# Attention outputs of two batches together, and the output products as seven products added in place

## The chip, the cores and the metric

The kernel runs on one core of one Trainium2 chip. The metric is device microseconds of one execution, from three runs before the change: a median of 2983.91 us, from 2983.39 to 2986.14.

A core has five engines that run side by side, each with its own queue, worked off in order: TensorE (PE in the profile; its weight loads are PEld), VectorE (DVE), ScalarE (ACT), GpSimd (POOL) and SyncE (SP), from which this kernel issues all its transfers. An instruction that needs another engine's result waits for a semaphore, and everything behind it in its own queue waits too. In this kernel TensorE's products go to tiles in PSUM, from where VectorE and ScalarE read them; everything else lies in SBUF.

## The reference

Two layers of masked attention with a residual and a normalisation each, over 128 batches of 128 rows and 512 columns in float32. Layer 0 has 4 heads and layer 1 has 8, each of 64 columns:

```python
q = split_heads(x @ Wq); k = split_heads(x @ Wk); v = split_heads(x @ Wv)
sim = jnp.einsum('bhid,bhjd->bhij', q, k) * scale
sim = jnp.where(adjacency_mask[:, None, :, :], sim, neg)
attn = jax.nn.softmax(sim, axis=-1)
out = jnp.einsum('bhij,bhjd->bhid', attn, v)          # heads joined: 256 columns
x = _layernorm(x + (out @ Wo + bo))                   # layer 0
# layer 1: h = layernorm(x) * gamma + beta, qkv = h @ w_qkv.T, 8 heads (512 columns),
# the mask also admits the diagonal
x = _layernorm(x + (out1 @ w_out.T + b_out))
```

The products that matter here are the last of each layer: `out @ Wo`, for each batch a 128x256 by 256x512 product in layer 0 and a 128x512 by 512x512 product in layer 1.

## The kernel before

Two batches make a group g (G = 2), so there are NG = 64 groups. The function `step(s)` works at several groups at once, as a pipeline: the projections of layer 0 for group s, attention of layer 0 for group s-1, the qk projection of layer 1 for group s-2, and attention of layer 1 for group s-3. A step has two halves, k = 2s and 2s+1, one for each batch of the groups. The order of instructions on every engine is the order in which the Python code issues them (a manual schedule): what stands earlier in `step` stands earlier in each engine's queue.

The projections are already formed by a scheme that multiplies two 2x2 block matrices with seven block products instead of eight. The left matrix's blocks are the two batches (rows) and the two halves of the inner dimension (columns); the right one's blocks are the halves of the weight. `sums` (L257) makes four sums of the left blocks on GpSimd (L266), the weights' sums are made once at the start (`weight_sums`, L160). `product` (L275) issues the products of layer 1 (kinds "qk" and "v", matmuls at L304) and `product_0` (L337) those of layer 0 (L361). The products are numbered 1 to 7, and the table `INTO` says to which accumulator each goes: 1, 6, 7 and 4 all run on in accumulator "a", 5 and 3 in "f", 2 in "c". The accumulator is read between them: after products 1, 5 and 6 ScalarE copies the partial sum out (`e`, `eqk`, `ev`; L330, L371), after 4 it copies the result (L332, L373), and after 2, 3 and 7 VectorE adds a copied partial sum and writes the result (L335, L376). A product that goes on in an accumulator has to wait until the copy of the one before it has been made.

In each half, for both layers: `scores(k)` makes the score products (L400) into four PSUM tiles, GpSimd fills the score tile with the masked value (L410), VectorE selects scores by the mask (L412), takes the row maxima (L415), and ScalarE makes the exponentials and their sums (L424). At its end `scores` calls `exponentials(1)`, which issues the exponentials of layer 0 at once; those of layer 1 wait for the next `exponentials()`. `normalised` has VectorE's reciprocal (L432) and GpSimd's multiplication (L433). `blocks` transposes the probabilities in 32x32 blocks (L448) and puts them out to memory (L198), `probs_arrive` fetches them back with the blocks in order (L204). `attend(k-1)` multiplies them with v (L471), half a step later, and copies the result (L474).

`residual` (L487) is the output product: for each batch and layer, two or four 128x512 matmuls into one PSUM tile (L493), then VectorE adds the residual (L499) and takes mean and variance (L501, L503), GpSimd makes the roots (L506 to L517), and `norms` (L522), issued by the next `flush()`, normalises on VectorE (L524). `addend` has prepared the residual with the bias (L483, L484). Layer 0's result is transposed (`turn`, L214), put out and fetched back (`arrive`), and `finish` (L245) scales it into layer 1's input; `in_order` does the same for x. Layer 1's result goes out (L528).

PSUM: a rotating pool of five tiles (`mm_tile`) serves scores, attention, the "c" accumulators and the output products; three single tiles serve the other accumulators ("a", "a0" and "f").

Of the kernel before, what the change touches and what calls it, by code (L numbers as in the profile page):

```python
# [17 lines left out]
P = 128  # L18
# [9 lines left out]
def kernel(ctx: ExitStack, tc: tile.TileContext, x, adj, wq, wk, wv, wo, bo,  # L28
# [13 lines left out]
    four = ctx.enter_context(tc.tile_pool(name="four", bufs=4))  # L42
    dram = ctx.enter_context(tc.tile_pool(name="dram", bufs=2, space=bass.MemoryType.DRAM))
    ps_mm = ctx.enter_context(tc.tile_pool(name="ps_mm", bufs=5, space=PSUM))
# [20 lines left out]
    X, M = {}, {}  # L65

    def load(g):
        if g >= NG:
            return
        X[g] = four.tile([P, G, E], F32, tag="x", name=f"x_{g}")  # L70
        M[g] = four.tile([P, G, N], U8, tag="m", bufs=6, name=f"m_{g}")
        nc.sync.dma_start(X[g], x[g * G:(g + 1) * G].rearrange("b n e -> n b e"))
        nc.sync.dma_start(M[g], adj[g * G:(g + 1) * G].rearrange("b i j -> i b j"))
# [8 lines left out]
    mhalf = const.tile([P, 2], F32, name="mhalf")  # L82
# [25 lines left out]

    spare = []
    for tag, n in (("qk1", 4), ("v1", 2), ("xT1", 2), ("xs1", 2)):  # L110
        rows_n = one.tile([P, n, E], F32, tag=tag, name=f"raw_{tag}")
        spare.extend(rows_n[:, i] for i in range(n))

    def load_transposed(dst, src, name, scaled=0):
        rows, cols = src.shape
        raws = []
        for r in range(rows // P):
            if not spare:
                raw = three.tile([P, cols], F32, tag="h", bufs=7, name=f"{name}_{r}")
            else:  # L120
                raw = spare.pop(0)
            nc.sync.dma_start(raw, src[r * P:(r + 1) * P, :])
            raws.append(raw)
# [36 lines left out]
    def weight_sums():  # L160
        for w, ws in ((w1qk, wsqk), (w1v, wsv)):
            for c in range(KH):
# [6 lines left out]
                t2, t3, t4 = ws[:, 0, c], ws[:, 1, c], ws[:, 2, c]  # L169
                nc.vector.tensor_sub(t3, b22, b12)  # L170
                nc.vector.tensor_sub(b12, b12, b11)
                nc.vector.tensor_sub(t2, b22, b12)
                nc.vector.tensor_sub(t4, b21, t2)

    def weight_sums_0():
        b11, b12, b21, b22 = (w0[:, c:c + KH, h].rearrange("p c t f -> p c (t f)")
                              for c in (0, KH) for h in range(2))
        t2, t3, t4 = (ws0[:, i].rearrange("p c t f -> p c (t f)") for i in range(3))
# [4 lines left out]

    weight_sums_0()
    load_transposed(w1, w_qkv, "w_qkv", scaled=INNER[1])
    setup.append(turn_gamma_beta)
    load_transposed(wo1, w_out, "w_out")
    setup.append(weight_sums)

    WO = (wo0, wo1)  # L190
    RATIO, H, XT, QK, V, QKV = {}, {}, {}, {}, {}, {}
# [14 lines left out]
    TURNED, SCR, RAW = {}, {}, {}  # L206

    def turn(l, g, b):
        if not 0 <= g < NG:
            return  # L210
        if b == 0:
            TURNED[l] = one.tile([P, 4, G * KC * 32], F32, tag=f"turned{l}", name=f"turned{l}_{g}")
        src = X[g][:, b] if l == 0 else H[g, b]
        nc.vector.transpose(TURNED[l].rearrange("p a (b c i) -> p a b c i", b=G, c=KC)[:, :, b],  # L214
                            src.rearrange("p (c a i) -> p a c i", a=4, i=32))
        if b == G - 1:
            SCR[l] = put(TURNED[l], f"scr{l}_{g}")

    def arrive(l, g):
        if not 0 <= g < NG:  # L220
            return
        RAW[l] = one.tile([P, 4, G, KC, 32], F32, tag=f"raw{l}", name=f"raw{l}_{g}")
        fetch(RAW[l].rearrange("p a b c i -> p a (b c i)"), SCR[l])

    def first_transposed():
        xT = XT[0, 0] = one.tile([P, KC, T], F32, tag="xT0", name="xT0_0")
        for b in range(G):
            pt = mm_tile(f"xt_{b}")
            for c in range(KC):
                nc.tensor.transpose(pt[:, c * N:(c + 1) * N], X[0][:, b, c * P:(c + 1) * P], ident)  # L230
# [26 lines left out]
    def sums(l, g):  # L257
        xT = XT[l, g]
        xs = one.tile([P, 4, KH, N], F32, tag=f"xs{l}", name=f"xs{l}_{g}")
        a = xT.rearrange("p (h c) (b n) -> p b h c n", h=2, b=2)  # L260
# [6 lines left out]
        XS[l, g] = xs  # L267
# [69 lines left out]
    def product_0(g, *which):  # L337
# [5 lines left out]
        for i in which:  # L343
# [10 lines left out]
            elif first:  # L354
                tag = {"a": "a0", "f": "f"}[bank]
                ACC[0, bank] = ps_st.tile([P, 512], F32, tag=tag, name=f"{bank}0_{g}")
# [273 lines left out]
```

## Time and profile before

| what | value |
|---|---|
| profiled execution, device time | 2984.46 us |
| its span, first to last instruction | 2982.7 us |
| time around the span | 1.8 us |
| mean granted TensorE clock | 0.994 of full speed |
| busy: PE / PEld | 2920.0 / 2402.9 us |
| busy: DVE / ACT / POOL | 1854.0 / 1334.2 / 1567.4 us |
| output matmuls (L493) | 1536 records, 713.2 us busy, mean 600 ns |
| period of a step in the steady part | 45.14 us |

A row of a timeline gives start and length in us, the engine, the line of kernel.py, the operation, what it writes and reads with partitions x elements, the number of instructions merged in the row, and in brackets for how long the engine sat idle ahead of it and who ended that wait. TensorE's records come in pairs: an fp32 matmul of the program leaves two, so "x4" on an output row of 128x512 is two matmuls of the program. Matmuls overlap and their ends are modelled, so the distance between two starts says what one costs.

### The profile page before, as it was taken

To read this page: it belongs to the slowest core of one execution; us is meant where nothing else is said; L and a number is where in the kernel's file an instruction comes from. 1 tells how busy PE (TensorE), PEld (TensorE's weight loads), DVE (VectorE), ACT (ScalarE), POOL (GpSimd) and SP (SyncE) were. 2 spreads that over 40 slices of the span, in tenths; PEclk is the share of its full clock that TensorE was granted. 3 is DMA by queue.
4 is the path that set the end of the run, shared out by engine and by line. 5 is a ranking of instruction groups with operands and counts; after the bars stand their busy time and mean duration, and the time that the engine had idled before them with its cause. 6 is when DMAs were issued, how large, how long until landed. Compare 5 with 4: busy or idle time off the path is not lost.

```text
span 2982.7 us, 59421 instructions
## 1 busy us (share of the span) xinstructions
PE 2920.0 (98%) x22089; PEld 2402.9 (81%) x22089; DVE 1854.0 (62%) x3291; ACT 1334.2 (45%) x4619; POOL 1567.4 (53%) x2055
## 2 busy tenths in 40 slices
PE   6899999999999999999999999999999999999997
PEld 5788888888888888888888888888888888888865
DVE  4466666666666666666656666666666666666654
ACT  2344444444444444444544444444444444444442
POOL 2455545545545555555555555455455455455543
PEclk8999999999999999999999999999999999999999
DMA  5454544544544544544544545545445445445332
GB/s 170 123 149 129 150 141 127 161 136 124 165 135 125 165 136 127 160 134 134 156 132 140 150 131 147 146 129 153 141 126 161 137 122 168 133 125 163 118 100 89
DMA packets 249136, 414.42 MB, mean 139 GB/s; under 512 B 41608, under 2 KB 181392, under 8 KB 248848
## 3 DMA queue, kind: packets, MB, share of 16 engines
q1 hardware_dynamic: 248848, 410.62, 46.3%
q8 instruction: 175, 2.87, 0.4%
q14 instruction: 113, 0.93, 0.1%
HBM read 209.72 MB, written 200.80 MB: 138 GB/s over the span
## 4 chain that ended last, share of the span: by engine, by line
PE 96%; DVE 1%; DMA 1%; ACT 1%; issue 0%; POOL 0%; SPq 0%; POOLq 0%; DVEq 0%; ACTq 0%
PE o L493 22%; PE qka L304 15%; PE a L361 12%; PE qkf L304 8%; PE va L304 8%; PE sc L400 6%; PE av L471 6%; PE f L361 6%; PE qkc L304 4%; PE vf L304 4%; PE c L361 3%; PE vc L304 2%; ACT sm L424 1%; DMA scrp<-turned 0%; DMA pT<-scrp 0%
## 5 line engine op out<-in xcount | busy, mean ns | idle before, releaser
L424 ACT ACTIVATE sm<-sm,nmax 128x128 f32<-128x128 f32 x1536 | 595.2, 389 | 618.6 <-DVE nmax L415 604.9
L493 PE MATMUL o<-wo,aT 128*128 128x512 f32 x1536 | 713.2, 600 | 10.0 <-ACT aT L474 10.0
L506 POOL TENSOR_SCALAR ve<-mv 128x1 f32<-128x1 f32 x256 | 57.0, 223 | 1133.0 <-DVE rec L432 798.8
L493 PEld LDWEIGHTS o<-wo,aT 128*128 128x128 f32 x1536 | 278.3, 191 | 269.3 <-issue 246.8
L433 POOL TENSOR_TENSOR sm<-sm,rec 128x512 f32<-128x512 f32 (+1 forms) x256 | 397.0, 1561 | 171.9 <-DVE rec L432 171.9
L412 DVE COPY_PREDICATED sm<-m,sc 128x512 f32<-128x512 uint8 (+1 forms) x512 | 271.0, 581 | 29.1 <-POOL sm L410 7.0
L424 ACT ACTIVATION_READ_ACCUMULATOR sm<-sm,nmax 128x1 f32 x1536 | 288.0, 187 | 0.0
L448 DVE STREAM_TRANSPOSE turned<-sm 128x512 f32<-128x512 f32 (+1 forms) x256 | 246.0, 965 | 45.0 <-POOL sm L433 45.0
L304 PE MATMUL qkf<-xs,w 128*128 128x128 f32 x2048 | 249.9, 275 | 0.1
L304 PE MATMUL qka<-xs,wsqk 128*128 128x128 f32 x2048 | 249.6, 275 | 0.0
L415 DVE TENSOR_REDUCE nmax<-sm 128x4 f32<-128x512 f32 (+1 forms) x256 | 244.0, 953 | 8.8
L304 PEld LDWEIGHTS qkf<-xs,w 128*128 128x128 f32 x2048 | 239.0, 192 | 0.6 <-POOL xs L266 0.4
L304 PEld LDWEIGHTS qka<-xs,wsqk 128*128 128x128 f32 x2048 | 239.0, 192 | 0.0
L524 DVE TENSOR_SCALAR h<-h,mv,rstd 128x512 f32<-128x512 f32 x128 | 70.0, 547 | 265.0 <-POOL rstd L513 265.0
L432 DVE RECIPROCAL rec<-total 128x4 f32<-128x4 f32 (+1 forms) x256 | 44.7, 175 | 296.6 <-ACT sm L424 296.6
L266 POOL TENSOR_TENSOR xs<-xT 128x256 f32<-128x256 f32 x256 | 186.0, 727 | 34.4 <-PE w_qkvt L129 14.5
L410 POOL MEMSET sm<- 128x512 f32 (+1 forms) x256 | 181.1, 735 | 1.4 <-DVE turned L448 1.3
L330 ACT COPY ev<-va 128x256 f32<-128x256 f32 x128 | 47.6, 372 | 298.7 <-PE va L304 298.7
L513 POOL TENSOR_TENSOR rstd<-ve,mhalf 128x2 f32<-128x2 f32 (+1 forms) x256 | 165.9, 648 | 21.3
L330 ACT COPY eqk<-qka 128x512 f32<-128x512 f32 x128 | 75.1, 587 | 214.4 <-PE qka L304 214.4
L484 POOL TENSOR_TENSOR h<-h,bias 128x512 f32<-128x512 f32 x128 | 162.7, 1271 | 7.0 <-ACT h L483 6.9
L484 POOL TENSOR_TENSOR x<-x,bias 128x512 f32<-128x512 f32 x128 | 162.2, 1267 | 0.0
(122 smaller groups left out, 5825.5 us busy)
## 6 DMA issues: line engine op xcount, KB each, us to landing
scrp<-turned SPq DMA_DIRECT2D x124, 768.0 KB, 3.3
pT<-scrp SPq DMA_DIRECT2D x496, 192.0 KB, 4.0
scr<-turned SPq DMA_DIRECT2D x127, 512.0 KB, 2.7
raw<-scr SPq DMA_DIRECT2D x508, 128.0 KB, 3.0
x<-in_x_dram SPq DMA_DIRECT2D x64, 512.0 KB, 4.2
out_dram<-y SPq DMA_DIRECT2D x128, 256.0 KB, 2.0
m<-in_adj_dram SPq DMA_DIRECT2D x64, 32.0 KB, 4.0
scrp<-turned SPq DMA_DIRECT2D x4, 512.0 KB, 3.2
```

The lines of the kernel that those rows point to most:

```text
L266: nc.gpsimd.tensor_tensor(o, a0, a1, op=op)
L304: nc.tensor.matmul(o, lhsT, rhs, start=first and n == 0, stop=n == len(todo) - 1, skip_group_check=True)
L361: nc.tensor.matmul(acc[:, t * P:(t + 1) * P], lhsT, rhs, start=first and n == 0, stop=n == len(todo) - 1, skip_group_check=True)
L400: nc.tensor.matmul(ps[h % 2][:, h // 2, :], q_, k_, start=True, stop=True)
L410: nc.gpsimd.memset(sm, (NEG0, NEG1)[l])
L412: nc.vector.copy_predicated(sm[:, s], mask[:, None, :].to_broadcast([P, K, N]), ps[s][:, :K, :])
L415: nc.vector.tensor_reduce(nmax, sm, AX.X, ALU.max, negate=True)
L424: nc.scalar.activation(sm[:, s, k, :], sm[:, s, k, :], AF.Exp, bias=nmax[:, s, k:k + 1], accum_out=total[:, s, k:k + 1])
L433: nc.gpsimd.tensor_tensor(sm, sm, rec[:, :, :, None].to_broadcast([P, 2, K, N]), op=ALU.mult)
L448: nc.vector.transpose(t[:, :, lo:hi, :], sm)
L484: nc.gpsimd.tensor_tensor(xin, xin, (bias0, bias1)[l], op=ALU.add)
L493: nc.tensor.matmul(pm, aT[:, c * P:(c + 1) * P], WO[l][:, c, :], start=(c == 0), stop=(c == nk - 1))
```

## The change

Attention of a group is now made for both batches at one place, `attend(s)`, for layer 0 of group s-2 and layer 1 of group s-4, so each layer's outputs come later by up to a step, and there is one more step. The output products take the same seven-product form as the projections (`out_product`): GpSimd makes the four sums of the attention outputs (`out_sums`), each product has one (layer 0) or two (layer 1) 128x256 matmuls, and after each product VectorE adds the accumulator, as it stands, into one quarter of the residual tile R, in place. The residual tile is the one in which x was loaded, and it stays one tile through both layers (six buffers of two batches). Mean and variance are taken per batch (`stats`), the roots for both batches together (`roots`); layer 1 is normalised on ScalarE (`norms_1`), layer 0 on VectorE (`norms_0`). The pool of rotating PSUM tiles has four tiles instead of five, and there is a fourth accumulator tile ("f0").

In `step` the order is new: product_0's parts stand between the output products of layer 0, both row transposes of a group are made together, product_0's number 7 and the statistics, `blocks`, normalisation and `turn` stand ahead of the second half's scores, and v's first four products stand behind these scores; the copies of their partial sums stand ahead of the exponentials of layer 1, and behind those of layer 0.

```diff
-    four = ctx.enter_context(tc.tile_pool(name="four", bufs=4))
+    six = ctx.enter_context(tc.tile_pool(name="six", bufs=6))
-    ps_mm = ctx.enter_context(tc.tile_pool(name="ps_mm", bufs=5, space=PSUM))
+    ps_mm = ctx.enter_context(tc.tile_pool(name="ps_mm", bufs=4, space=PSUM))
...
+    spare = []
+    def spare_rows(pool, tag, n):
+        rows_n = pool.tile([P, n, E], F32, tag=tag, name=f"raw_{tag}_{len(spare)}")
+        spare.extend(rows_n[:, i] for i in range(n))
+    for i in range(4):
+        spare_rows(six, "r", 2)
+    for tag, n in (("qk1", 4), ("v1", 2), ("xT1", 2)):
+        spare_rows(one, tag, n)
-        X[g] = four.tile([P, G, E], F32, tag="x", name=f"x_{g}")
-        M[g] = four.tile([P, G, N], U8, tag="m", bufs=6, name=f"m_{g}")
-        nc.sync.dma_start(X[g], x[g * G:(g + 1) * G].rearrange("b n e -> n b e"))
+        R[g] = six.tile([P, G, E], F32, tag="r", name=f"r_{g}")
+        M[g] = six.tile([P, G, N], U8, tag="m", name=f"m_{g}")
+        nc.sync.dma_start(R[g], x[g * G:(g + 1) * G].rearrange("b n e -> n b e"))
...
+    WSO = tuple(const.tile([P, 3, i // P // 2, E // 2], F32, name=f"wso{l}") for l, i in enumerate(INNER))
+    def weight_sums_out(l):
+        hk = INNER[l] // P // 2
+        w = (wo0, wo1)[l]
+        combine(*(w[:, c:c + hk, h * E // 2:(h + 1) * E // 2] for c in (0, hk) for h in range(2)),
+                *(WSO[l][:, i] for i in range(3)))
...
+    setup.append(weight_sums)
+    setup.append(lambda: weight_sums_out(0))
-    setup.append(weight_sums)
+    setup.append(lambda: weight_sums_out(1))
...
+    def turn(l, g):
+        if not 0 <= g < NG:
+            return
+        t = one.tile([P, 4, G * KC * 32], F32, tag="turned_in", name=f"turned{l}_{g}")
+        for b in range(G):
+            nc.vector.transpose(t.rearrange("p a (b c i) -> p a b c i", b=G, c=KC)[:, :, b],
+                                R[g][:, b].rearrange("p (c a i) -> p a c i", a=4, i=32))
+        SCR[l] = put(t, f"scr{l}_{g}")
+        RAW[l] = one.tile([P, 4, G, KC, 32], F32, tag="raw", name=f"raw{l}_{g}")
...
+        xs = XS[l, g] = one.tile([P, 4, KH, N], F32, tag=f"xs{l}", name=f"xs{l}_{g}")
+        halves_sums(xs, XT[l, g].rearrange("p (h c) (b n) -> p b h c n", h=2, b=2))
+    def halves_sums(xs, a):
         s1, s2, s3, s4 = (xs[:, i] for i in range(4))
         for o, a0, a1, op in ((s1, a[:, 1, 0], a[:, 1, 1], ALU.add),
                               (s2, s1, a[:, 0, 0], ALU.subtract),
                               (s4, a[:, 0, 1], s2, ALU.subtract),
                               (s3, a[:, 0, 0], a[:, 1, 0], ALU.subtract)):
             nc.gpsimd.tensor_tensor(o, a0, a1, op=op)
-        XS[l, g] = xs
...
-                tag = {"a": "a0", "f": "f"}[bank]
-                ACC[0, bank] = ps_st.tile([P, 512], F32, tag=tag, name=f"{bank}0_{g}")
+                ACC[0, bank] = ps_st.tile([P, 512], F32, tag=f"{bank}0", name=f"{bank}0_{g}")
-                e = one.tile([P, 512], F32, tag=("e5_0" if i == 5 else f"e{i}"), name=f"e0_{i}_{g}")
-                EV[0, i] = e[:, :3 * P]
+                EV[0, i] = one.tile([P, 3 * P], F32, tag=f"e0_{i}", name=f"e0_{i}_{g}")
...
+    def out_product(l, g, *which):
+        if not 0 <= g < NG:
+            return
+        aT, so = AT[l, g], SO[l, g]
+        hk = INNER[l] // P // 2
+        w, ws = WO[l], WSO[l]
+        EH = E // 2
+        for i in which:
+            left = {1: aT[:, 0, :hk], 2: aT[:, 0, hk:], 3: so[:, 3], 4: aT[:, 1, hk:], 5: so[:, 0],
+                    6: so[:, 1], 7: so[:, 2]}[i]
+            right = {1: w[:, :hk, :EH], 2: w[:, hk:, :EH], 3: w[:, hk:, EH:], 4: ws[:, 2],
+                     5: w[:, :hk, EH:], 6: ws[:, 0], 7: ws[:, 1]}[i]
+            bank, first = INTO[i]
+            if first and bank == "c":
+                ACC["o", bank] = mm_tile(f"oc{l}_{g}")
+            elif first:
+                ACC["o", bank] = ps_st.tile([P, 512], F32, tag=(bank, f"{bank}0")[l], name=f"o{bank}{l}_{g}")
+            acc = ACC["o", bank][:, :EH]
+            for c in range(hk):
+                nc.tensor.matmul(acc, left[:, c], right[:, c], start=first and c == 0, stop=c == hk - 1,
+                                 skip_group_check=True)
+            b, h = {1: (0, 0), 2: (0, 0), 6: (0, 1), 3: (0, 1), 5: (1, 1), 7: (1, 1), 4: (1, 0)}[i]
+            part = R[g][:, b, h * EH:(h + 1) * EH]
+            nc.vector.tensor_add(part, acc, part)
...
+        pT = one.tile([P, 4, sum(HEADS), 32], F32, tag="pT", bufs=2, name=f"pT_{k}")
...
+    def attend(s):
+        for l, g in ((0, s - 2), (1, s - 4)):
+            if not 0 <= g < NG:
+                continue
             K = HEADS[l] // 2
+            aT = AT[l, g] = one.tile([P, G, K, N], F32, tag=f"aT{l}", name=f"aT{l}_{g}")
+            for b in range(G):
+                pT = PT.pop((l, g, b))
+                if l == 1 or b == 0:
+                    pm = mm_tile(f"av{l}_{g}_{b}").rearrange("p (k n) -> p k n", n=N)
+                for h in range(HEADS[l]):
+                    i, kk = h % 2, h // 2
+                    o = pm[i * D:(i + 1) * D, (b * K if l == 0 else 0) + kk, :]
+                    v = (QKV[g][:, b, kk, 2, i * D:(i + 1) * D] if l == 0
+                         else V[1, g][:, b, h * D:(h + 1) * D])
+                    nc.tensor.matmul(o.rearrange("p (a r) -> p a r", r=32), v, pT[:, :, i * K + kk, :],
+                                     start=True, stop=True)
+                if l == 1:
+                    nc.scalar.copy(aT[:, b], pm)
+                elif b == G - 1:
+                    nc.scalar.copy(aT.rearrange("p b k n -> p (b k) n"), pm)
+    def out_sums(l, g):
+        if not 0 <= g < NG:
+            return
+        K = HEADS[l] // 2
+        so = SO[l, g] = one.tile([P, 4, K // 2, N], F32, tag=("so", "xs0")[l], name=f"so{l}_{g}")
+        halves_sums(so, AT[l, g].rearrange("p b (h c) n -> p b h c n", h=2))
...
+    def addend(l, g):
+        if not 0 <= g < NG:
+            return
+        if l == 1:
+            for b in range(G):
+                nc.scalar.activation(R[g][:, b], R[g][:, b], AF.Copy, scale=RATIO[g][:, b:b + 1])
+        nc.gpsimd.tensor_tensor(R[g], R[g], (bias0, bias1)[l][:, None, :].to_broadcast([P, G, E]),
+                                op=ALU.add)
+    MV = {}
+    def stats(l, g, b):
+        if not 0 <= g < NG:
+            return
+        if b == 0:
+            MV[l, g] = two.tile([P, G, nc.vector.BN_AGGR_DIM], F32, tag="mv", name=f"mv{l}_{g}")
+        st = three.tile([P, nc.vector.BN_STATS_DIM], F32, tag="st", name="st")
+        nc.vector.bn_stats(st, R[g][:, b])
+        nc.vector.bn_aggr(MV[l, g][:, b], st)
+        if b == G - 1:
+            roots(l, g)
+    def roots(l, g):
+        mv = MV[l, g]
+        n = 2 - l
+        ve = two.tile([P, 2, G], F32, tag="ve", name=f"ve{l}_{g}")
+        nc.gpsimd.tensor_scalar_add(ve[:, 0], mv[:, :, 1], EPS)
+            nc.gpsimd.tensor_scalar(ve[:, 1], mv[:, :, 1], 1.0 + EPS, EPS * EPS, op0=ALU.mult,
+                                    op1=ALU.add)
+        root = two.tile([P, 2, G], F32, tag="root", name=f"root{l}_{g}")
+        nc.gpsimd.tensor_tensor(root[:, :n].rearrange("p i b -> p (i b)"),
+                                ve[:, :n].rearrange("p i b -> p (i b)"), mhalf[:, :n * G], op=ALU.pow)
+        if l == 0:
+            ratio = RATIO[g] = three.tile([P, G], F32, tag="ratio", bufs=5, name=f"ratio_{g}")
+            nc.gpsimd.tensor_tensor(ratio, ve[:, 1], root[:, 1], op=ALU.mult)
+            nc.gpsimd.tensor_tensor(ratio, ratio, root[:, 0], op=ALU.mult)
+            later.append(lambda: norms_0(g, mv, root))
+            shift = two.tile([P, G], F32, tag="shift", name=f"shift_{g}")
+            nc.gpsimd.tensor_tensor(shift, mv[:, :, 0], root[:, 0], op=ALU.mult)
+            nc.gpsimd.tensor_scalar_mul(shift, shift, -1.0)
+            later.append(lambda: norms_1(g, shift, root))
+    def norms_0(g, mv, root):
+        for b in range(G):
+            nc.vector.tensor_scalar(R[g][:, b], R[g][:, b], mv[:, b, 0:1], root[:, 1, b:b + 1],
+                                    op0=ALU.subtract, op1=ALU.mult)
+    def norms_1(g, shift, root):
+        for b in range(G):
+            nc.scalar.activation(R[g][:, b], R[g][:, b], AF.Identity, bias=shift[:, b:b + 1],
+                                 scale=root[:, 0, b:b + 1])
+        nc.sync.dma_start(out[g * G:(g + 1) * G].rearrange("b n e -> n b e"), R[g])
...
     def step(s):
...
         k = 2 * s
+        if s:
+            load(s + 1)
         scores(k)
-        addend(0, k - 1)
-        residual(1, k - 2)
+        addend(0, s - 2)
         p("qk", 4, g=s - 3)
+        product_0(s, 1)
         exponentials()
-        attend(k - 1)
+        attend(s)
+        out_sums(0, s - 2)
         normalised(k)
-        addend(1, k - 1)
-        flush()
-        turn(0, s + 1, 0)
-        turn(0, s + 1, 1)
-        product_0(s, 1, 5)
+        product_0(s, 5)
+        p("", g=-1)
+        product_0(s, 2)
+        addend(1, s - 4)
+        p("", g=-1)
+        out_product(0, s - 2, 1, 5, 2, 6)
+        product_0(s, 6)
+        p("", g=-1)
+        out_product(0, s - 2, 3)
+        stats(0, s - 2, 0)
+        out_product(0, s - 2, 7)
+        product_0(s, 3)
+        p("", g=-1)
+        out_product(0, s - 2, 4)
+        product_0(s, 7)
+        stats(0, s - 2, 1)
         p("", g=-1)
         blocks(k)
-        arrive(0, s + 1)
-        product_0(s, 2, 6)
-        p("", g=-1)
-        product_0(s, 3)
-        residual(0, k - 1)
+        flush()
+        turn(1, s - 2)
+        arrive(1, s - 2)
         probs_arrive(k)
-        p("v", 1, 5, g=s - 3)
-        flush()
-        turn(1, s - 2, 1)
-        p("v", 2, 6, g=s - 3)
-        arrive(1, s - 2)
-        p("v", 3, g=s - 3)
-        load(s + 2)
         k += 1
         scores(k)
-        addend(0, k - 1)
-        p("v", 7, g=s - 3)
-        residual(1, k - 2)
+        product_0(s, 4)
+        out_sums(1, s - 4)
+        p("v", 1, 5, g=s - 3)
+        p("v", 2, 6, g=s - 3)
         exponentials()
+        out_product(1, s - 4, 1)
+        p("v", 3, 7, g=s - 3)
+        normalised(k)
+        out_product(1, s - 4, 5, 2)
         p("v", 4, g=s - 3)
-        attend(k - 1)
-        normalised(k)
-        addend(1, k - 1)
+        finish(s - 2)
+        turn(0, s + 1)
+        out_product(1, s - 4, 6)
+        blocks(k)
+        out_product(1, s - 4, 3)
+        stats(1, s - 4, 0)
+        out_product(1, s - 4, 7)
+        arrive(0, s + 1)
+        probs_arrive(k)
+        p("qk", 1)
+        p("qk", 5)
+        out_product(1, s - 4, 4)
+        stats(1, s - 4, 1)
+        p("qk", 2)
+        in_order(s + 1)
+        p("qk", 6)
         flush()
-        finish(s - 2)
-        product_0(s, 7)
-        blocks(k)
-        residual(0, k - 1)
-        product_0(s, 4)
-        in_order(s + 1)
-        p("qk", 1)
-        probs_arrive(k)
-        flush()
-        turn(1, s - 1, 0)
-        p("qk", 5)
-        p("qk", 2, 6)
         p("qk", 3, 7)
     first_transposed()
-    for s in range(NG + 3):
+    for s in range(NG + 4):
         step(s)
-    k = 2 * (NG + 3) - 1
-    residual(1, k - 1)
-    attend(k)
-    addend(1, k)
-    residual(1, k)
-    flush()
```

## The prediction

> **What bounds the kernel now.** I read the page's busy shares first, then the chain that ended last, then TensorE's own timeline over one period, then the other engines' timelines at the places the diff touches.
>
> Busy shares, and the chain's shares by line, from the page:
>
> ```profile
> PE 2920.0 (98%) x22089; PEld 2402.9 (81%) x22089; DVE 1854.0 (62%) x3291; ACT 1334.2 (45%) x4619; POOL 1567.4 (53%) x2055
> ...
> PE o L493 22%; PE qka L304 15%; PE a L361 12%; PE qkf L304 8%; PE va L304 8%; PE sc L400 6%; PE av L471 6%; PE f L361 6%; PE qkc L304 4%; PE vf L304 4%; PE c L361 3%; PE vc L304 2%; ACT sm L424 1%; DMA scrp<-turned 0%; DMA pT<-scrp 0%
> ```
>
> TensorE sets the time, and the largest line on it is the one that the change rewrites. TensorE's timeline repeats every 45.14 us (scores of a step start at 1454.93 and 1500.07); from 135 us on TensorE has no idle. Piece of that timeline (start, length, line):
>
> ```profile
> 1475.44 1.03 PE L304 MATMUL vf<-w,xs 128*128 128x256 f32 x4
> 1476.40 0.71 PE L400 MATMUL sc<-qkv 64*128 64x128 f32 x8
> 1476.95 1.06 PE L400 MATMUL sc<-qk 64*128 64x128 f32 x16
> 1477.94 1.13 PE L304 MATMUL va<-wsv,xs 128*128 128x256 f32 x4
> 1478.90 3.60 PE L493 MATMUL o<-wo,aT 128*128 128x512 f32 x8
> 1482.34 1.03 PE L304 MATMUL va<-wsv,xT 128*128 128x256 f32 x4
> ```
>
> I price TensorE from start to start: a v product (two 128x256 matmuls) 0.86 us, four 128x512 output matmuls 3.44, so 0.43 per 256 columns; scores 0.54 + 0.98; from other rows likewise qk product 1.79, layer 0 product 1.34 to 1.45, attention of one batch 0.49 + 0.97.
>
> Durations of VectorE (DVE) and ScalarE (ACT) in the same period:
>
> ```profile
> 1472.91 0.69 DVE L501 BATCH_NORM_STATS2 st<-h 128x6 f32<-128x512 f32 x1
> 1475.23 0.55 DVE L524 TENSOR_SCALAR h<-h,mv,rstd 128x512 f32<-128x512 f32 x1 [1.40 <-POOL rstd L513]
> 1475.81 0.71 DVE L214 STREAM_TRANSPOSE turned<-h 128x512 f32<-128x512 f32 x1
> 1477.21 0.78 DVE L412 COPY_PREDICATED sm<-m,sc 128x256 f32<-128x256 uint8 x2
> 1478.02 0.69 DVE L415 TENSOR_REDUCE nmax<-sm 128x4 f32<-128x512 f32 x1
> 1486.40 0.56 DVE L376 TENSOR_TENSOR qkv<-a,e 128x384 f32<-128x384 f32 x1
> ```
> ```profile
> 1473.05 0.37 ACT L330 COPY ev<-va 128x256 f32<-128x256 f32 x1 [3.39 <-PE va L304]
> 1478.80 0.40 ACT L424 ACTIVATE sm<-sm,nmax 128x128 f32<-128x128 f32 x1 [2.79 <-DVE nmax L415]
> 1489.45 0.48 ACT L373 COPY qkv<-a 128x384 f32<-128x384 f32 x1 [0.95 <-PE a L361]
> ```
>
> Here the select (L412) starts 0.81 after its scores; ev is copied as soon as its product is there, before any exponential of this half.
>
> [...]the trace has 0.41 for v adds of 256 and 0.69 for 512. [...]the trace has L524 at 507 to 2110 ns.
>
> **The change, part by part, per step of two batches.**
>
> 1. Output matmuls. Removed: 12 of 128x512, 10.4 us (3.53 + 3.44 + 1.72 + 1.71). Added: 7x1 + 7x2 of 128x256 at 0.43: 9.1. Gain 1.3; a full step is 43.8 of TensorE work.
> 2. In-place adds: 14 at 0.41, 5.8, for four residual adds, 2.7. In the first half nearly hidden: product 6 may overwrite the bank of product 1 only after its add, which follows the reciprocal (exponentials end about 8.5 into the step), the qkv add (11.1) and itself (11.4); TensorE gets there at 11.8. Margin only 0.4; product 4 waits some 0.1.
> 3. New sums on GpSimd: four of 128x128 (0.45 each, extrapolated from 0.73 at 256 and 1.27 at 512) and four of 128x256 (0.73): 4.7. They start 9.1 into the step, and the first is needed 1.8 later: hidden. If late, each microsecond is TensorE's.
> 4. Attention of both batches (2.9 us together) at one place: probabilities of the second half should land some 8 us before use (put 3.3, fetch 4.0): hidden. Loads a step earlier: same number, hidden. Outputs: one 512 KB issue for two of 256 KB. Layer 1's normalisation to ScalarE, 2 x 0.6, after qk copies: hidden. Power on 128x4: about 1.0 (0.58 for one, 0.72 for two columns), hidden behind 1.8 of transposes.
> 5. Order of the step's middle. VectorE's queue now has, after layer 0's product 7 and before the second half's selects: qkv add, statistics of the second batch, both probability transposes, both normalisations, both row transposes. From the end of product 7 (T), start to start: semaphore 0.27, add 0.47, statistics 0.73, aggregate 0.15, transposes 1.82, normalisations 0.43 + 0.58, turns 0.63 + 0.65: the select starts at T+5.7 instead of T'+0.8 after its scores.
>    TensorE after T: scores 1.5, product 4 1.34, v products 1 and 5 1.73: at T+4.6 it needs for v product 2 the buffer of the first select (four rotating buffers now, and the uses per step are 16, so the slots repeat): free at T+6.1. Wait 1.5.
>    ScalarE's queue: layer 0's four exponentials stand ahead of the qkv copy and of ev 1. Only those of layer 1 come after. Exponentials start at T+5.7+1.6 = 7.3, take 1.56, copy 0.37, ev 1 0.37: T+9.7. v product 6 accumulates into the bank that ev 1 reads. Without waits TensorE would be there at T+5.5. The total wait is 4.2.
>    After it TensorE has work in stock; I followed the rest (exponentials of layer 1, reciprocals, adds, finish, qk) and found each due before its turn by 0.3 us or more, so nothing gives the 4.2 back.
> 6. The clock. The 4.2 fall into gaps of 1.5 and 2.7 with 0.9 of work between. What a gap of 2.9 did in the ramp (granted clock is the third number from the end; TensorE's busy time the first after the length):
>
> ```profile
> 123.00:126.00 3.00, 0.19 (x1) 0.00 (x0) 2.83 (x6) 1.74 (x9) 0.00 (x0) 1.00 0.78 229
> 126.00:128.00 2.00, 1.87 (x12) 1.49 (x14) 0.16 (x2) 2.00 (x11) 1.04 (x1) 0.81 0.32 89
> 128.00:130.00 2.00, 2.00 (x21) 1.67 (x17) 0.20 (x1) 1.55 (x8) 0.59 (x1) 0.50 0.77 179
> ```
>
>    That cost 1.7 us (126.13 to 131.26 holds 3.4 of work). Gaps of 2.3 at 70 and 2.55 at 2903 did it too, those of 2.6 at 2863 and 2.3 at 2922 did not: three of five, so about 1.0 per step. Bounds: 0 and 1.7.
> 7. Ends. One more step, and the last output passes sums, seven products and roots: from the last probabilities on some 7 more; the half-empty last steps have less work to cover the same chain: 5 to 15 more; the start waits less for probabilities (7 us of such gaps before 66 us), say 5 to 10 less. Net +10, from -5 to +25.
>
> Sum: a step becomes 43.8 + 4.2 + 1.0 = 49.0, +3.9 on 45.14. Sixty steps are full (145.6 to 2854.5): 60 x 3.9 = 234, +10. On the profiled execution, span 2982.7 and 1.8 around it, 2984.5: 3228. Its own time lies 0.6 above the median of the runs, 2983.9. I round the clock term down a little, since the second gap may be shorter than its sum: 3215.
>
> **Rivals.**
> - The wait is there but the clock holds: 60 x 2.9 + 10 gives 3168; with 0.5 less of chain 3138. For it: two of five gaps. Against: two gaps close together.
> - The clock halves in every step: 60 x 4.6 + 10 gives 3270. [...]
> - Faster: the middle chain is covered. TensorE's gain of 1.34 a step then stays: 2984.5 - 80 + 10 = 2914. Place: between layer 0's product 7 and v product 6. It decides for faster where the chain takes less than 6.8 us (5.5 of cover and 1.3 of gain) against my 9.7. Against it: nearly all of the 9.7 is durations in this trace on two queues that keep order; 2.9 of error is needed.
> - More waits: product 6 of layer 0 missing its 0.4, or a normalisation blocked by GpSimd as L524 at 2110 ns: 0.5 to 1.5 per step on top, 3250 to 3310. For it: narrow margins. Against: GpSimd is then at small root operations and a memset.
>
> **How the numbers follow.** Wait with some halving, 3180 to 3260: 0.55; wait with a clock that holds or a shorter wait, 3080 to 3180: 0.22; halving in each step or more waits, above 3260: 0.15; covered, about 2914: 0.08. The likeliest is 3215. The range 3110 to 3285 leaves out the covered case, the tail of long waits and that of short ones. Within 0.2% is about what a measurement of this kernel can tell from no change; only a chain near 6.8 us lands there: 0.02. Faster 0.06, slower 0.92.
>
> **What would show it.** Step period 49 us (45.1 before). TensorE waiting at v products (line 312 of the changed kernel) for VectorE's select and above all for ScalarE's ev copy, some 1.5 and 2.7 us a step, 250 us over the run, and the first exponential of the second half starting 7 us after layer 0's product 7. TensorE's clock at 0.5 for up to 3.4 us after it. Output groups 9.1 us a step. Wrong if TensorE has no idle at line 312, or if its waits sit at the output products (then part 2 was misjudged) or at attention (part 4).

## The result, and the profile after

The changed kernel takes 3312.89 us (median of four, 3295.32 to 3317.29) against 2984.45 before: ratio 1.109, 95% interval 1.105 to 1.113. The prediction, 3215 with a range up to 3285, had the direction and missed the size by 98 us. The profiled execution took 3313.47 us, its span 3311.0, at a mean granted clock of 0.948 (before 0.994).

The page of the changed kernel, busy shares first, then the chain that ended last:

```profile
PE 3000.8 (91%) x23241; PEld 2708.0 (82%) x23241; DVE 2053.3 (62%) x3811; ACT 1408.7 (43%) x4683; POOL 1732.3 (52%) x2247
...
PE 63%; DVE 17%; ACT 8%; DMA 4%; issue 3%; POOL 2%; SPq 1%; ACTq 0%; DVEq 0%; POOLq 0%
```

TensorE still has the largest share, but it is no longer nearly the whole chain (96% before): a quarter runs through VectorE and ScalarE. ("issue" is time in which an engine waited for nothing that the profile shows.) In the rows below, `va`, `vf` and `vc` are the accumulators of v's products, `oa`, `of` and `oc` those of the output products, and `sm` is the score tile. TensorE's waits, longest totals first (what waited, for whom, us in total, times, longest):

```profile
PE va L312 <- ACT ev L338: 143.1, 63, 2.6
PE vc L312 <- DVE sm L444: 80.6, 62, 2.9
PE a L368 <- ACT xT L249: 17.1, 2, 10.6
PE qka L312 <- ACT xT L260: 12.3, 2, 11.4
```

Two waits come once in every step, at the v products; the other two belong to the start. Here is the middle of one step, from the timeline of all engines. T, the end of layer 0's product 7, is 1634.09, where the second half's scores begin:

```profile
1634.19 0.56 DVE L382 TENSOR_TENSOR qkv<-a,e 128x384 f32<-128x384 f32 x1 [0.91 <-PE a L368]
...
1637.28 1.34 DVE L571 TENSOR_SCALAR r<-r,mv,root 128x512 f32<-128x512 f32 x2
...
1638.54 1.28 DVE L223 STREAM_TRANSPOSE turned<-r 128x512 f32<-128x512 f32 x2
...
1639.76 0.73 DVE L444 COPY_PREDICATED sm<-m,sc 128x256 f32<-128x256 uint8 x2
...
1640.21 1.13 PE L312 MATMUL vc<-w,xT 128*128 128x256 f32 x4 [1.25 <-DVE sm L444]
...
1641.32 0.40 ACT L456 ACTIVATE sm<-sm,nmax 128x128 f32<-128x128 f32 x1 [10.89 <-DVE nmax L447]
...
1642.88 0.45 ACT L379 COPY qkv<-a 128x384 f32<-128x384 f32 x1
1643.24 0.36 ACT L338 COPY ev<-va 128x256 f32<-128x256 f32 x1
...
1643.65 2.07 PE L312 MATMUL va<-wsv,xs 128*128 128x256 f32 x4 [2.31 <-ACT ev L338]
...
1645.52 1.91 PE L404 MATMUL oa<-wo,aT 128*128 128x256 f32 x4
```

The select starts at T+5.67 and v product 6 at T+9.56; the prediction had T+5.7 and T+9.7. ScalarE sat idle for 10.89 us before its first exponential, and yet the ev copy that TensorE needs came after four of them. The last two rows show the second effect: the output product starts 1.87 us after the v product, where such a product takes 0.86 at full clock. TensorE's clock in the same place, by windows (the third number from the end is the granted clock, the first after the length is TensorE's busy time):

```profile
1639.47:1642.88 3.41, 1.13 (x4) 0.68 (x4) 3.24 (x7) 1.56 (x9) 2.92 (x5) 1.00 0.53 215
1642.88:1646.30 3.42, 2.65 (x6) 2.17 (x7) 2.09 (x3) 1.53 (x6) 0.00 (x0) 0.50 0.75 193
1646.30:1649.71 3.41, 3.41 (x9) 2.66 (x8) 0.85 (x2) 2.91 (x16) 0.00 (x0) 0.50 0.99 191
1649.71:1653.12 3.41, 3.41 (x17) 2.98 (x16) 2.03 (x7) 0.14 (x1) 2.08 (x2) 1.00 0.00 0
```

From 1642.88 on the clock is at half for 6.83 us. These windows are not chosen freely: in this trace the granted clock changes only at the borders of one grid of 3.413 us (to within 0.01 us), and each window above is one cell of it. Over the sixty steps in which every stage of the pipeline has work, a cell tells what the next one gets. Of 60 cells at full clock in which TensorE was busy for less than half (0.29 to 0.49 of the cell), 55 were followed by half clock. The other five, at 0.43 to 0.45, and the 743 cells with 0.51 or more were followed by full clock. Of the 79 cells at half clock, the 24 that were busy for 0.82 or less were followed by another one, the 55 with 0.83 or more by full clock.

From start to start of a step's first scores, the mean of the sixty full steps is 50.16 us (before 45.15). The shortest is 47.85: work and waits with no slow clock. The second half, from its scores on, takes 29.98 us in 5 steps of the 60, 31.4 to 31.7 in 29, and up to 33.8 in the other 26. Five steps have no cell at half clock, 31 have one and 24 have two. The mean of the second half is 32.04, 2.06 more than without; half of TensorE's busy time in the cells at half clock is 1.97 of it. The first half takes 17.87 in many steps and 18.12 in the mean, which is another 0.25 (explained below). Outside the sixty, the start is 15.5 us longer (the fifth step's scores come at 161.12 instead of 145.58) and the tail 12.4 (140.5 after the last full step, 128.1 before). 60 x 5.01 + 15.5 + 12.4 gives 328.5 against a difference of the spans of 328.3.

### The profile page after: what moved, and what is told of

It is laid out like the page before. It is cut to its first block, busy times and chain, and to the rows that moved or that the text cites. A ratio compares the mean times of both kernels' runs of the same rounds, so it can differ in the third digit from the quotient of the medians.

```text
span 3311.0 us, 62490 instructions
## 1 busy us (share of the span) xinstructions
PE 3000.8 (91%) x23241; PEld 2708.0 (82%) x23241; DVE 2053.3 (62%) x3811; ACT 1408.7 (43%) x4683; POOL 1732.3 (52%) x2247
## 4 chain that ended last, share of the span: by engine, by line
PE 63%; DVE 17%; ACT 8%; DMA 4%; issue 3%; POOL 2%; SPq 1%; ACTq 0%; DVEq 0%; POOLq 0%
PE oa L404 11%; PE qka L312 10%; PE a L368 7%; PE va L312 7%; ACT sm L456 6%; PE qkf L312 5%; PE of L404 5%; PE f L368 4%; DVE turned L480 4%; PE av L507 3%; DVE sm L444 3%; DVE nmax L447 3%; DMA raw<-scr 3%; PE vf L312 3%; PE qkc L312 3%
## 5 line engine op out<-in xcount | busy, mean ns | idle before, releaser
L465 POOL TENSOR_TENSOR sm<-sm,rec 128x512 f32<-128x512 f32 (+1 forms) x256 | 370.8, 1469 | 497.8 <-DVE rec L464 497.8
L408 DVE TENSOR_TENSOR r<-oa,r 128x256 f32<-128x256 f32 x512 | 213.3, 417 | 311.7 <-PE oa L404 291.7
L275 POOL TENSOR_TENSOR so<-aT 128x128 f32<-128x128 f32 (+1 forms) x256 | 154.6, 604 | 431.4 <-ACT aT L512 431.4
L312 PE MATMUL va<-wsv,xs 128*128 128x256 f32 x512 | 186.8, 500 | 143.1 <-ACT ev L338 143.1
L528 POOL TENSOR_TENSOR r<-r,bias 128x1024 f32<-128x1024 f32 x128 | 301.6, 2356 | 4.2 <-ACT r L527 4.2
L312 PEld LDWEIGHTS va<-wsv,xs 128*128 128x128 f32 x512 | 125.7, 258 | 191.3 <-ACT ev L338 168.7
L404 PE MATMUL of<-wo,so 128*128 128x256 f32 x768 | 214.3, 388 | 4.3 <-POOL so L275 3.0
L404 PE MATMUL oa<-wso,so 128*128 128x256 f32 x768 | 210.3, 383 | 0.2 <-DVE r L408 0.2
L548 POOL TENSOR_SCALAR ve<-mv 128x2 f32<-128x2 f32 x128 | 28.3, 221 | 338.2 <-DVE mv L540 338.2
L539 DVE BATCH_NORM_STATS2 st<-r 128x6 f32<-128x512 f32 x256 | 177.2, 692 | 6.7
```

Source lines behind the costliest of these rows:

```text
L275: nc.gpsimd.tensor_tensor(o, a0, a1, op=op)
L312: nc.tensor.matmul(o, lhsT, rhs, start=first and n == 0, stop=n == len(todo) - 1, skip_group_check=True)
L404: nc.tensor.matmul(acc, left[:, c], right[:, c], start=first and c == 0, stop=c == hk - 1, skip_group_check=True)
L408: nc.vector.tensor_add(part, acc, part)
L465: nc.gpsimd.tensor_tensor(sm, sm, rec[:, :, :, None].to_broadcast([P, 2, K, N]), op=ALU.mult)
L528: nc.gpsimd.tensor_tensor(R[g], R[g], (bias0, bias1)[l][:, None, :].to_broadcast([P, G, E]), op=ALU.add)
```

## The experiments

The theory that came out of this reading: two queue orders cause the waits (VectorE's statistics, normalisations and transposes ahead of the second half's select; ScalarE's exponentials of layer 0 ahead of the ev copies), and the half clock that follows from the waits costs about half as much again. Rivals: the clock is slow for some other reason; or removing one wait only moves it to the next. V product 2 waits for the select because it needs the score tile that the select reads, in a pool of four tiles where there were five; no run here changed that number. All diffs are against the changed kernel, except where said.

### ScalarE's order alone

The copies of partial sums and the qkv copy go ahead of layer 0's exponentials.

```diff
-    def scores(k):
+    def scores(k, left=1):
...
-        exponentials(1)
+        exponentials(left)
...
         k += 1
-        scores(k)
+        scores(k, 2)
         product_0(s, 4)
         out_sums(1, s - 4)
         p("v", 1, 5, g=s - 3)
+        exponentials(1)
         p("v", 2, 6, g=s - 3)
```

> ScalarE's order alone: the copies ev 1, ev 5 and the qkv copy stand ahead of layer 0's exponentials in the second half. Theory A (one chain, from layer 0's product 7 over VectorE's queue and the exponentials to the ev copy, then the halved clock): v product 6 no longer waits, v product 2 still waits about 1.3 us for the select, the second gap is gone and with it nearly all of the halved clock. Step 45.2 instead of 50.2 us, about 3015 us in all (60 x 5.0 less than 3313). Theory B (the output products' new form costs it: small matmuls, in-place adds, four rotating tiles instead of five): none of that is changed, so over 3250 us.

Measured 3128.68 us, ratio 1.048 (1.047 to 1.050), clock 0.989. The wait for ev is gone, and with it the slow clock: 184 us, more than the 143 of that wait. Of the sixty steps 58 stay at full clock; in the other two the wait for the select was 2.13 and 2.91 us. The expected 3015 was not reached. TensorE's waits in this kernel:

```profile
PE vc L312 <- DVE sm L444: 82.1, 62, 2.9
PE oa L404 <- DVE r L408: 48.6, 63, 2.5
PE of L404 <- DVE r L408: 24.6, 59, 0.6
```

The wait for the select stays as it was, 1.25 us in most steps, now alone, and with this one gap the clock stays at full in 58 of the 60 steps. New are waits at layer 1's output products, some 1.2 us a step: the adds of products 5 and 2 stand on VectorE behind the reciprocal of layer 1's sums (`normalised`), and that waits for exponentials which now come later than TensorE. So this order was one of the causes, and the rival that a removed wait moves on holds in part as well.

### VectorE's order alone

```diff
         out_product(0, s - 2, 4)
-        product_0(s, 7)
         stats(0, s - 2, 1)
         p("", g=-1)
         blocks(k)
+        product_0(s, 7)
         flush()
...
         scores(k)
+        p("v", 1, 5, g=s - 3)
         product_0(s, 4)
         out_sums(1, s - 4)
-        p("v", 1, 5, g=s - 3)
         p("v", 2, 6, g=s - 3)
```

> VectorE's order alone: statistics of the second batch and both probability transposes stand ahead of layer 0's product 7 and its add; layer 0's product 4 stands behind v products 1 and 5. The exponentials of layer 0 still stand ahead of the ev copies. Theory A: the select starts some 1.25 us sooner, v product 2 waits about 0.3, v product 6 about 2.3 us; one gap in place of two, with a halved clock in part of the steps (0 to 1.7 us). Step 46.4 to 48.1 us, total 3085 to 3190. Theory B: no change, over 3250.

Measured 3292.48 us, ratio 1.103 (1.101 to 1.105), clock 0.953: a miss, with both waits nearly as before (120.5 and 95.5 us in total). The select starts 5.99 us after its scores. The statistics had moved ahead, and the normalisations behind them start 0.94 us sooner, but take longer by more than that: 2.60 us for the two instead of 1.34. The next run shows it in the trace.

### Both orders

The two diffs together, with v's products 1 and 5 right behind the scores.

> Both orders together. Theory A: waits of 0.3 us at v product 2 and none at v product 6, clock full; step 44.1 us, so 60 x 6.05 less than 3313: about 2950 us, which is below the kernel before (2984). Theory B: over 3200, since all output products, in-place adds and tiles are as in the changed kernel.

Measured 3110.02 us, ratio 1.042 (1.041 to 1.044): a miss again, only 19 us better than ScalarE's order alone. The wait for the select is even longer, 1.6 us a step. VectorE and GpSimd at the same time in this kernel:

```profile
1631.25 2.61 DVE L571 TENSOR_SCALAR r<-r,mv,root 128x512 f32<-128x512 f32 x2
1631.31 1.42 POOL L442 MEMSET sm<- 128x512 f32 x2
1632.68 0.90 POOL L275 TENSOR_TENSOR so<-aT 128x256 f32<-128x256 f32 x1
```

Two normalisations, priced at 1.01 from the kernel before, take 2.61 while GpSimd fills the score tiles and starts its sums. Over this trace one such operation takes from 0.53 to 1.76 us. In the kernel before, the 128 of layer 0 had only a small GpSimd operation (L517) beside them and took 0.55 each; of the 128 of layer 1, 126 stood beside the multiplication of the probabilities (L433) and took 0.51 to 2.11. Both reorderings start the normalisations earlier, and both put them into this fill.

### The same, with layer 0 normalised on ScalarE

If GpSimd's work beside them is the cause, moving the two normalisations off VectorE must free the select, and by more than the 1.01 us that they were priced at. The rival is a queue that is simply full, where something else takes their place. Against the kernel with both orders (the ratio for the next addend is formed after `shift`):

```diff
-    def norms_0(g, mv, root):
-        for b in range(G):
-            nc.vector.tensor_scalar(R[g][:, b], R[g][:, b], mv[:, b, 0:1], root[:, 1, b:b + 1],
-                                    op0=ALU.subtract, op1=ALU.mult)
+        # l is 0 or 1; root[:, 1] is layer 0's scale
+        i = 1 - l
+        shift = two.tile([P, G], F32, tag=f"shift{l}", name=f"shift{l}_{g}")
+        nc.gpsimd.tensor_tensor(shift, mv[:, :, 0], root[:, i], op=ALU.mult)
+        nc.gpsimd.tensor_scalar_mul(shift, shift, -1.0)
+        later.append(lambda: norms(l, g, shift, root[:, i]))
...
+            nc.scalar.activation(R[g][:, b], R[g][:, b], AF.Identity, bias=shift[:, b:b + 1],
+                                 scale=scale[:, b:b + 1])
```

> As e3_both, with layer 0's normalisation on ScalarE in place of VectorE (two operations of 128x512 there, two small ones on GpSimd for the shift). In e3_both the two normalisations on VectorE took 2.61 us in the steady step where two such operations cost 1.0 when GpSimd is quiet. Theory A' (they are blocked by GpSimd's memset and sums, and this holds up the select and v product 2 by 1.6 us): the select starts about 4.4 us after the scores of the second half instead of 6.0, v product 2 waits at most 0.2; step about 45.3 instead of 46.7, total about 3025. Rival (VectorE's queue is simply full there and something else takes the place): step 46.4 or more, total 3090 or more.

Measured 3048.92 us, ratio 1.022 (1.021 to 1.024); the expected 3025 was not quite reached. The wait for the select, in the kernel with both orders and in this one:

```profile
PE vc L312 <- DVE sm L444: 99.5, 62, 3.2
PE vc L312 <- DVE sm L444: 16.5, 62, 3.5
```

It falls by 83 us, and the time by 61. The select starts 4.63 us after its scores instead of 6.00, that is 1.37 sooner, although the row transposes now wait 0.97 for ScalarE. A queue relieved of 1.01 us of work explains less than that. So this run fits a slowdown beside GpSimd, but since it takes work off VectorE too, it doesn't test that alone. The wait of layer 1's output products stays (`oa` 50.2 us in total).

### Is the slow clock a cost of its own?

The changed kernel with its orders untouched, but with useless work put into the two gaps: v product 5 is made three times and v product 2 four times, into the same tiles with the same result. That is 5 x 0.86 = 4.3 us of added TensorE work per step.

```diff
+            for o, lhsT, rhs, c in todo * {5: 2, 2: 3}.get(i, 0):
+                nc.tensor.matmul(o, lhsT, rhs, start=c == 0, stop=c == KH - 1, skip_group_check=True)
```

> The changed kernel, with the two gaps filled by work that has no use: v product 5 is made three times and v product 2 four times in place (same result), 4.3 us more of TensorE work per step. If the halved clock after the gaps is what lies between my 47.9 us of work and waits and the measured 50.2, then the clock stays full, and a kernel with more work is faster: step 48 to 48.8 us, total 3185 to 3230. If the clock is not it (other waits make up the rest), the step stays at 50.2 or above, total 3310 or more.

Measured 3206.37 us, ratio 1.074 (1.073 to 1.076), clock 0.991. More work makes the changed kernel 106 us faster. No cell of the sixty steps is at half clock, and in none is TensorE busy for less than 0.65. The most frequent period is 48.06 us, which is 43.8 of work and the 4.3 added. The v products of this kernel, and the output product between them, follow one another at 0.86:

```profile
1641.27 1.03 PE L314 MATMUL va<-wsv,xs 128*128 128x256 f32 x4
1642.13 1.03 PE L406 MATMUL oa<-wo,aT 128*128 128x256 f32 x4
1642.99 1.03 PE L314 MATMUL vf<-w,xs 128*128 128x256 f32 x4
```

So the half clock comes from TensorE's idle time here, and it costs what the profile of the changed kernel says: about 2 us a step. That answers the rival of another reason for the slow clock.

### The start

The start's waits are for transposed rows, which the changed order turns, puts out and fetches later in the step than before. In the first two steps, the turn of x is moved to the first half:

```diff
         product_0(s, 2)
+        if s < 2:
+            turn(0, s + 1)
+            arrive(0, s + 1)
         addend(1, s - 4)
...
-        turn(0, s + 1)
+        if s >= 2:
+            turn(0, s + 1)
...
-        arrive(0, s + 1)
+        if s >= 2:
+            arrive(0, s + 1)
```

> The changed kernel with x of groups 1 and 2 transposed and fetched in the first half of steps 0 and 1 instead of the second. If the two waits of TensorE for these rows in the first 72 us (6.6 and 10.6 us) are what makes the start 15.5 us longer than before, some 10 to 15 us go: about 3300. If another wait of the ramp takes their place, the total stays at 3313 within its spread.

Measured 3310.6 us (3304.67 to 3320.57), which overlaps the changed kernel's own runs: inconclusive in time. In the trace the fifth step starts 4.2 us sooner, while a wait of 8.1 us for a select takes the place of part of the 17.1 that went. The rest of the start was not taken apart.

### All orders mended

To see what the change is worth without its queues, the following was put together: layer 0's normalisation on ScalarE; GpSimd's fill of the score tiles half a step ahead; layer 0's select and maxima ahead of the row transposes; both orders from above; the addend of layer 0 in the half before; layer 1's products 6, 3 and 7 together; the copies of the next x behind the qk copies; the early turns of the first steps. What each of these gives alone was not tried. Its core (`between` holds layer 1's row transposes and is called after layer 0's select and maxima):

```diff
+            if between:
+                between()
+                between = None
...
-        exponentials(1)
+        exponentials(left)
...
         blocks(k)
+        product_0(s, 7)
         flush()
-        turn(1, s - 2)
-        arrive(1, s - 2)
-        probs_arrive(k)
+        clear(k + 1)
+        def between():
+            turn(1, s - 2)
+            arrive(1, s - 2)
+            probs_arrive(2 * s)
         k += 1
-        scores(k)
+        scores(k, 2, between)
+        p("v", 1, 5, g=s - 3)
         product_0(s, 4)
         out_sums(1, s - 4)
-        p("v", 1, 5, g=s - 3)
+        exponentials(1)
```

> All orders mended: as e5, and the row transposes of layer 1's input stand between the selects of layer 0 and layer 1; the fills of the score tiles are issued a half step sooner; layer 0's addend is made a half step sooner; output products 6, 3 and 7 of layer 1 stand together ahead of the transposes of the next x; x's copies stand behind the qk copy; in the first two steps x is transposed early. Theory A: no wait of TensorE left in a full step, so the seven-product form keeps its 1.3 us: step 43.8 to 44.3, total 2915 to 2950, below the kernel before. Theory B (the form costs more than it gains): not below 2984.

Measured 2976.75 us (eight runs), ratio 0.998 (0.997 to 0.999): a gain, but less than expected. Its period is 44.63, and one wait that comes in every step is left, seen in its timeline:

```profile
1614.56 0.20 DVE L476 RECIPROCAL rec<-total 128x8 f32<-128x8 f32 x1 [1.93 <-ACT sm L468]
...
1615.19 1.10 PE L404 MATMUL of<-wo,so 128*128 128x256 f32 x4 [0.60 <-DVE r L408]
```

### The last wait

It is the wait that the first experiment had shown. From the kernel just above, one line is moved:

```diff
-        normalised(k)
         out_product(1, s - 4, 5, 2)
+        normalised(k)
         p("v", 4, g=s - 3)
```

> The kernel with all orders mended (2976.8 us, period 44.63) has one wait left in each step: TensorE 0.60 us at layer 1's output product 3, for the in-place add of product 5, which stands on VectorE behind the reciprocal of layer 1's sums, and that waits 1.93 for ScalarE's exponentials. Here the reciprocals and their multiplications of the second half come after the adds of products 5 and 2. If that order is all that holds the add, the wait goes and nothing takes its place: period 44.0, 2940 us (2932 to 2950). Rival: the probabilities are multiplied later on GpSimd, so their transposition and VectorE's queue behind it, or the fetch for the next step's attention, come late instead: then the wait moves to layer 1's output products 6 and 4 or to the attention (line 519), and the time stays at 2970 to 2985.

Measured 2937.26 us (2935.94 to 2938.60), ratio 0.984 (0.983 to 0.986): as expected, and faster than both kernels. VectorE's queue in this kernel, where the adds of products 5 and 2 now come first and the reciprocal still waits, but for nobody's harm:

```profile
1593.79 0.42 DVE L408 TENSOR_TENSOR r<-of,r 128x256 f32<-128x256 f32 x1
1594.13 0.42 DVE L408 TENSOR_TENSOR r<-oc,r 128x256 f32<-128x256 f32 x1
1594.47 0.17 DVE L476 RECIPROCAL rec<-total 128x4 f32<-128x4 f32 x1
1595.89 0.20 DVE L476 RECIPROCAL rec<-total 128x8 f32<-128x8 f32 x1 [1.25 <-ACT sm L468]
```

TensorE is 94% of its chain again, and the mean period is 44.02 (43.8 to 44.0 in two thirds of the steps). Against the kernel before: 60 x 1.13 gained, start 10.4 and tail 10.6 lost, 47 us in all.

## Why the prediction was right or wrong, point by point

- **Part 1, output matmuls: right.** The work of a step was put at 43.8 us. The last kernel above, which has hardly any waits left, comes to 43.85 most often, 1.3 less than before.
- **Part 2, in-place adds: right for layer 0.** Product 6 didn't wait (the add of product 1 began at 1627.29 in the step shown, product 6 at 1627.98), product 4 waits under 0.2. For layer 1 the adds are close to a wait, which shows as soon as the bigger waits are gone.
- **Parts 3 and 4, sums and moved work: right but for one cost.** "Hidden" held for attention, transfers and sums. Not seen was how much longer VectorE takes beside GpSimd in the first half. The larger addend (one operation on 128x1024) runs beside the maximum of the mask and the diagonal, which took 0.28 us before. Before, then after:

```profile
1457.14 0.28 DVE L407 TENSOR_TENSOR m<-m,eye 128x128 uint8<-128x128 uint8 x1
...
1617.41 2.35 POOL L528 TENSOR_TENSOR r<-r,bias 128x1024 f32<-128x1024 f32 x1
...
1618.04 1.87 DVE L439 TENSOR_TENSOR m<-m,eye 128x128 uint8<-128x128 uint8 x1
```

  In the sixty full steps it takes 1.27 to 1.92 us there. Up to 1.48 the first half stays at 17.87; above, it grows by at least as much as the maximum does: 1.61 and less gives mostly up to 18.0, 1.70 gives 18.10, 1.90 gives 18.3 to 18.5. That is the 0.25 per step. In the last two kernels, where the addend stands elsewhere, the first half takes 17.83 in all sixty steps, and the maximum in this place 0.28 (at 1630.90 in the first of the two). Of the changed kernel's own 128, the six with no GpSimd instruction beside them took 0.28, and those of the second half beside the sums of the attention outputs 0.40 to 0.84. The prediction had named a slowdown beside GpSimd in a rival, for the normalisation alone, and counted the memset there as harmless; beside it the two took 0.25 longer (1.26 for 1.01, from start to start).
- **Part 5, the order in the middle: right**, nearly to the instruction. Both waits, at the places named, total 4.0 us from start to start (47.85 less 43.85) for 4.2. That the times agree to 0.15 us is partly luck: in the T+5.7, an add that starts 0.10 after T instead of 0.27 makes up for normalisations of 1.26 from start to start instead of 1.01, and the terms of the T+9.7 add up to 9.6.
- **Part 6, the clock: wrong in size; this is the term that failed.** It was put at 1.0 a step, at most 1.7. Measured: 2.06. The first error was to read the five gaps of the trace before as chances, three in five. In these windows, again cells of a grid of 3.413 us, the first three are those that were followed by half clock:

```profile
69.21:72.62 3.41, 1.11 (x10) 0.95 (x9) 1.61 (x4) 2.65 (x11) 1.04 (x1) 1.00 0.01 2
123.83:127.24 3.41, 1.11 (x6) 0.73 (x6) 2.30 (x5) 2.15 (x11) 0.94 (x1) 1.00 0.44 151
2902.28:2905.69 3.41, 1.18 (x22) 0.94 (x18) 0.00 (x0) 3.41 (x18) 0.58 (x1) 1.00 0.00 0
2861.32:2864.73 3.41, 1.70 (x27) 1.34 (x25) 0.20 (x2) 3.13 (x15) 1.80 (x3) 1.00 0.00 0
2919.34:2922.76 3.42, 1.96 (x21) 1.33 (x19) 2.35 (x5) 3.02 (x12) 1.51 (x3) 1.00 0.55 153
```

  TensorE was busy for about 0.33 of the cell in those three, and for 0.50 and 0.57 in the two that stayed at full clock. Waits of 1.25 and 2.31 with 1.13 of busy time between them leave a cell below half nearly wherever they fall on the grid, so 55 of 60 steps lost something. The second error was the bound: 1.7 is what one cell at half clock costs, and 24 steps have two, because the first was not busy enough. The rival "halves in every step" was nearer, and its 3270 still too low, in part for this second reason.
- **Part 7, the ends: wrong in sign for the start**, +15.5 for -5 to -10. The fewer waits for probabilities were counted, and the later turn of the rows, which TensorE waits for while the pipeline is still filling (29.4 us in all, against 3.5 before), was not. Turning those of two groups early won back 4.2 us, so where the rest of the start goes stays open. The tail, +12.4, was inside 12 to 22.

The 98 us: clock 60 x 1.06 = 64; rounding the sum down, 13; the mask's maximum 15; ends 18; the wait shorter by 0.2, -12. Together 98.

## What to carry to other kernels

An order written out by hand has to be read per queue: here ScalarE sat idle for 10.89 us ahead of an exponential, with the ev copy that TensorE needed behind it, and the orders of the queues, and which engine normalises, lay between a loss of 10.9% and a gain of 1.6%. Price a wait on TensorE with the clock that follows it: here waits worth 4.0 us in two pieces cost 2 us more, and useless work in the gaps was faster than the gaps. Look in your own trace for what the clock follows; here it was how much of each cell of a 3.413 us grid was idle. When VectorE's operations are moved, look at what GpSimd does in the new place: here two normalisations took 2.61 us for 1.01 beside its fill and its sums.

## What was not expected of the hardware

- TensorE at half clock for 6.83 us after two gaps of 1.25 and 2.31 us. None of the waits at these two places was longer than 2.9. In the sixty steps the clock of the next cell went with the busy share of a cell of 3.413 us: with 0.42 or less it was always half, with 0.51 or more never, and between them both happened. At half clock it took a share of 0.83 to come back, which is 0.41 of what full clock could do. TensorE's busy time is modelled, so these limits are estimates from this trace.
- A 128x128 uint8 maximum on VectorE took up to 1.92 us for 0.28 beside a GpSimd addition of 2.35, and two normalisations took 2.61 for 1.01 beside a memset and a sum.
